# A transformer layer with folded butterflies on one core: where the down side's fold ends, and which engine writes the up side's diagonal matrices

## The chip, the core and the metric

The kernel runs on one core of a Trainium2 chip. The time is device microseconds (us) for one launch. PE is TensorE (matmuls), DVE is VectorE, ACT is ScalarE, POOL is GpSimd, and SP issues most DMAs. Each engine takes its instructions in the order of the program.

## What is computed

A batch of 16 sequences (512 tokens, width 256) goes through causal attention with 16 heads (rotary positions, low-rank additions to wq and wv), a layer norm, a feed-forward block with butterflies, and a second layer norm:

```python
h = einsum('bsd,dh->bsh', x, W_exp) + b_exp          # 256 -> 1024
h = butterfly(h, up_weights, 1024)                   # 10 stages
h = gelu(h + up_bias)
h = butterfly(h, down_weights, 1024)                 # 10 stages
y = einsum('bsh,hd->bsd', h, W_con) + b_con          # 1024 -> 256
```

A butterfly is linear, so the kernel multiplies each of the two into its neighbouring weight matrix once, while the first sequences run: `W_exp` with the up butterfly, `W_con` with the down butterfly. This is the **fold**. After it the feed-forward block is two plain products with the folded weights `wup` and `wdn`.

## The kernel before, in words

The main loop walks through slots `s` from -2 on. Every sequence has 20 slots, in four groups of five (`u` = 0 to 4). From slot 15 on, a slot does two things: the score products of the current sequence's `weights` (line 479, into the PSUM tile `pb`, then exp on ACT at line 493 and a mask on POOL at line 497), and the score products of `largest`, 15 slots ahead (line 421, into `pa`, then row maxima on DVE at line 430). `pb` and `pa` exist once each. So the next slot's `pb` products wait for this slot's exp, and the next `pa` products for this slot's maxima. Behind these come what `others[s]` and `holes` hold for the slot: products with the probabilities (`po`, line 521), projections of later sequences (`pqk`, `pvv`), normalizing (lines 553 and 554), the output projection (`pwo`), and the feed-forward block. Sequence 0 has its first expansion products (`hidden`, line 633, `ph`) in slots 46 to 49, two per slot, its gelus in slot 50, and its first contraction (`contract`, line 660, reads `wdn`) in slot 51.

The fold's tasks are run last in each slot, by a list with a number of tasks due per slot. A task has a `begin`, run up to two tasks ahead, and a second half. The kinds, by side (0 is up, on `ya`; 1 is down, on `wdn`):

- `all_within`: six `multiply_paths` on DVE (line 215) build a matrix of 128x128 per chunk from the factors of seven stages; then eight `within_chunk`, each a matmul (line 219) and an ACT copy (line 222).
- `all_across` by `across_by_products` (up side, stages 7 and 8): per pair of chunks, `begin` writes four diagonal matrices `d` by scaling `ident` (line 255); the second half is four matmuls (line 267) and two ACT copies (line 272).
- `all_across` by `across_chunks` (up side stage 9, down side stages 9, 8, 7): `begin` is two ACT scalings (line 232, tiles `x`, four buffers); the second half is two DVE operations (line 239) on two tensors of SBUF each.
- `up_done` (lines 294 and 295): transposes the folded up side into `wup`.

The up side's `within` runs in slots 2 to 14. Slots 15 to 44 spread the other 44 tasks evenly: 12 across pairs and all 14 `within` tasks of the down side, mixed with 12 across pairs and two small sums of the up side, and four `up_done` at the end. `wup` shares its memory (`yb`) with the down side's factors `factors[1]`, so the down side's `within` has to be over before `up_done` writes.

PSUM for all other products is a ring of three banks (`ps_w`), and `fold`, `pd`, `ptw`, `pt1`, `ph`, `pwo` take turns in it.

Of the kernel before, what the change touches and what calls it, by code (L numbers as in the profile page):

```python
# [11 lines left out]
F32 = mybir.dt.float32  # L12
BF16 = mybir.dt.bfloat16
AF = mybir.ActivationFunctionType
ALU = mybir.AluOpType
PSUM = bass.MemoryType.PSUM

P = 128
# [5 lines left out]
NSP = 7  # L24
# [9 lines left out]
def decoder_layer(  # L34
# [18 lines left out]
    nc = tc.nc  # L53
    B, T, D = x.shape
# [3 lines left out]
    NHC = DHID // P  # L58
    DA = D + 1
    NQ = NC * 2  # L60

    const = ctx.enter_context(tc.tile_pool(name="const", bufs=1))
# [11 lines left out]
    def bank(name, shape):  # L74
        return ps_w.tile(shape, F32, tag="w", name=name)
# [25 lines left out]
    ya = early[:, 0 : NHC * DA].rearrange("p (c d) -> p c d", d=DA)  # L101
    nfac = NHC * (2 * P - 2)
    factors = [early[:, NHC * DA : NHC * DA + nfac], None]
# [4 lines left out]
    coefs = const.tile([P, 2, NS - NSP, NHC, 2], F32, name="coefs")  # L108
    ubias = const.tile([P, NHC], F32, name="ubias")
    wdn = const.tile([P, NHC, D], F32, name="wdn")  # L110
    bias2 = const.tile([P, 2, D], F32, name="bias2")

    yb = const.tile([P, NHC * DA], F32, name="yb")
    wup = yb[:, 0 : NC * DHID].rearrange("p (c e) -> p c e", c=NC)
    factors[1] = yb[:, 0:nfac]


    def load_more(n):
# [86 lines left out]
    def multiply_paths(side, r):  # L205
        m = 1 << r
        if side == 0:
            cur = block(side, r).rearrange("p (c two m) -> p c two m", c=NHC, two=2)
            prev = block(side, r - 1).rearrange("p (c o m) -> p c o m", c=NHC, o=1)
            prev = prev.to_broadcast([P, NHC, 2, m])  # L210
        else:
            cur = block(side, r).rearrange("p (c m two) -> p c m two", c=NHC, two=2)
            prev = block(side, r - 1).rearrange("p (c m o) -> p c m o", c=NHC, o=1)
            prev = prev.to_broadcast([P, NHC, m, 2])
        nc.vector.tensor_tensor(cur, cur, prev, ALU.mult)

    def within_chunk(side, c, y, cols):
        pb = bank(f"fold_{side}_{c}", [P, cols])
        nc.tensor.matmul(
            pb, block(side, NSP - 1)[:, c * P : (c + 1) * P], y[:, c, :], start=True, stop=True  # L220
        )
        nc.scalar.copy(y[:, c, :], pb)
# [23 lines left out]
    def across_by_products(side, s, c, y, cols):  # L246

        pair = (c, c ^ (1 << (s - NSP)))
        parts = {}

        def begin():
            for one in pair:
                d = small.tile([P, 2, P], F32, tag="diag", name=f"d_{side}_{s}_{one}", bufs=4)
                for i in range(2):
                    nc.scalar.activation(
                        d[:, i, :],
                        ident,
                        AF.Identity,
                        scale=coefs[:, side, s - NSP, one, i : i + 1],
                    )  # L260
                parts[one] = d

        def rest():
            for one, other in (pair, pair[::-1]):
                ps = bank(f"pd_{side}_{s}_{one}", [P, cols])
                for i, chunk in enumerate((one, other)):
                    nc.tensor.matmul(
                        ps, parts[one][:, i, :], y[:, chunk, :], start=(i == 0), stop=(i == 1)
                    )
                parts["ps", one] = ps  # L270
            for one in pair:
                nc.scalar.copy(y[:, one, :], parts["ps", one])

        return begin, rest

    def all_across(side, y, cols):

        stages = range(NSP, NS) if side == 0 else range(NS - 1, NSP - 1, -1)
        for s in stages:
            for c in range(NHC):  # L280
                if not c & (1 << (s - NSP)):
                    by = across_by_products if side == 0 and s < NS - 1 else across_chunks
                    yield by(side, s, c, y, cols)

    def mixed(one, two):

        one, two = list(one), list(two)
        keyed = [((i + 0.5) / len(q), n, t) for n, q in enumerate((one, two)) for i, t in enumerate(q)]
        return [t for _, _, t in sorted(keyed, key=lambda k: k[:2])]

    def up_done(d, half):
        pt = bank(f"ptw_{d}_{half}", [P, 4, P])
        for n in range(4):
            nc.tensor.transpose(pt[:, n, :], ya[:, 4 * half + n, d * P : (d + 1) * P], ident)
        nc.vector.tensor_copy(
            wup[:, d, half * 4 * P : (half + 1) * 4 * P],
            pt.rearrange("p n q -> p (n q)"),
        )
# [4 lines left out]
    def all_within(side, y, cols):  # L303
        for r in range(1, NSP):
            yield idle, lambda r=r: multiply_paths(side, r)
        for c in range(NHC):
            yield idle, lambda c=c: within_chunk(side, c, y, cols)

    def fold_tasks():
        def up():  # L310
            yield from all_across(0, ya, DA)
            yield idle, lambda: nc.vector.tensor_add(
                hbias, ya[:, :, D : D + 1].rearrange("p c o -> p (c o)"), ubias
            )
            yield idle, lambda: nc.vector.tensor_add(
                bias2[:, 0, :], bias2[:, 0, :], bias2[:, 1, :]
            )

        def down():
            yield from all_across(1, wdn, D)  # L320
            yield from all_within(1, wdn, D)


        last = [
            (idle, lambda d=d, half=half: up_done(d, half))
            for d in range(NC)
            for half in range(2)
        ]
        return list(all_within(0, ya, DA)), mixed(down(), up()) + last


    def project(b, side, c):
# [352 lines left out]
    per = PER_QUAD * NQ  # L685
    behind = PER_QUAD * BEHIND
    end = B * per + behind
    last = end + 8
# [23 lines left out]
    for b in range(B):  # L712
        s = b * per
# [33 lines left out]
        if b + 2 < B:  # L747

            late = 2 * (b + 3 == B)
# [54 lines left out]
        add(end + 7, finish_tile, z, t)  # L804


    first, second = fold_tasks()
    fold = first + second
    tasks_at = dict(zip(range(2, behind), (0, 1, 2, 3, 4, 4, 5, 5, 5, 6, 9, 11, 14)))
    for s in range(behind, 2 * per + 5):  # L810
        tasks_at[s] = len(first) + -(-len(second) * (s - behind + 1) // (2 * per + 5 - behind))
    ahead = 0
    given = 0
    due = deque()
# [173 lines left out]
```

## Time and profile before

| what | value |
|---|---|
| median of 3 runs | 1359.33 us (1358.64 to 1360.84) |
| profiled execution, its time / its span | 1357.15 us / 1355.4 us |
| PE, DVE, ACT, POOL busy over the span | 1320.3, 925.8, 707.3, 510.9 us |
| first 40:60, 60:80, 100:120 us, PE busy of 20 | 17.85, 16.57, 17.39 us |
| 180:200 us and 220:240 us, PE busy of 20 | 20.00, 19.97 us |
| line 255 (`d`), line 239 (two-tensor operations of the across tasks) | 32 and 32 instructions, all between 56 and 136 us |

PE is busy 97% of the span, and almost all of its idle time lies in the first 170 us, where the fold runs. To read the slots in time: slot 15 begins at 55.4 us (its first `pb` product), slot 26 at 93.4, slot 34 at 122.0, slot 45 at 166.2, slot 50 at 189.8. In the profile, PE's matmuls in fp32 appear as two records each.

### The profile page before, as it was taken

To read this page: it belongs to the slowest core of one execution; us is meant where nothing else is said; L and a number is where in the kernel's file an instruction comes from. 1 tells how busy PE (TensorE), PEld (TensorE's weight loads), DVE (VectorE), ACT (ScalarE), POOL (GpSimd) and SP (SyncE) were. 2 spreads that over 40 slices of the span, in tenths; PEclk is the share of its full clock that TensorE was granted. 3 is DMA by queue.
4 is the path that set the end of the run, shared out by engine and by line. 5 is a ranking of instruction groups with operands and counts; after the bars stand their busy time and mean duration, and the time that the engine had idled before them with its cause. 6 is when DMAs were issued, how large, how long until landed. Compare 5 with 4: busy or idle time off the path is not lost.

```text
span 1355.4 us, 23859 instructions
## 1 busy us (share of the span) xinstructions
PE 1320.3 (97%) x8728; PEld 702.5 (52%) x8728; DVE 925.8 (68%) x2949; ACT 707.3 (52%) x1079; POOL 510.9 (38%) x777
## 2 busy tenths in 40 slices
PE   8898999999999999999999999999999999998998
PEld 4453545455454545555454554545555454554555
DVE  4788757667685766758577685857768685776632
ACT  2575454454646445464645545464554546445643
POOL 3534215344251533425153352515335252531311
PEclk9998999999999999999999999999999999999999
DMA  5311010110102011010110101010110101000000
GB/s 172 120 45 45 22 59 30 40 45 30 68 30 74 30 41 45 30 67 30 67 35 31 57 30 68 30 60 30 40 60 30 68 30 55 30 27 32 30 12 31
DMA packets 45685, 63.49 MB, mean 47 GB/s; under 512 B 5752, under 2 KB 26232, under 8 KB 45568
## 3 DMA queue, kind: packets, MB, share of 16 engines
q1 hardware_dynamic: 41680, 56.42, 11.8%
q10 hardware_dynamic: 3888, 5.55, 1.3%
q8 instruction: 69, 1.13, 0.3%
q14 instruction: 48, 0.39, 0.1%
HBM read 23.40 MB, written 8.91 MB: 24 GB/s over the span
## 4 chain that ended last, share of the span: by engine, by line
PE 84%; DVE 11%; ACT 3%; issue 2%; DMA 0%; POOLq 0%; POOL 0%; DVEq 0%; SPq 0%; ACTq 0%
PE pb L479 19%; PE ph L633 17%; PE py L660 16%; PE po L521 10%; PE pqk L337 8%; DVE junk L430 5%; PE pvv L383 4%; PE pwo L559 3%; PE pa L421 3%; DVE bn L577 1%; PE pb L421 1%; PE pt L616 1%; ACT pT L493 1%; PE pa L479 1%; DVE z L567 1%
## 5 line engine op out<-in xcount | busy, mean ns | idle before, releaser
L430 DVE CUSTOM_DVE_ANT_0 junk<-pa,causal 128x384 bf16<-128x384 f32 (+2 forms) x878 | 438.3, 499 | 235.0 <-PE pa L421 176.1
L493 ACT ACTIVATE pT<-pb 128x1024 f32<-128x1024 f32 (+1 forms) x314 | 293.8, 936 | 377.3 <-PE pa L421 227.6
L497 POOL TENSOR_SCALAR_AFFINE_SELECT pT<-pT 128x256 f32<-128x256 f32 x512 | 202.5, 407 | 733.3 <-ACT pT L493 731.6
L479 PE MATMUL pb<-qz,kz 17*128 17x512 f32 (+2 forms) x1756 | 328.8, 473 | 16.1 <-ACT pT L493 12.1
L421 PE MATMUL pa<-kz,qz 32*128 32x384 f32 (+3 forms) x1756 | 329.2, 474 | 4.2 <-DVE mx L430 4.2
L660 PE MATMUL py<-wdn,h 128*128 128x256 f32 x1024 | 252.1, 391 | 0.0
L479 PEld LDWEIGHTS pb<-qz,kz 17*128 17x128 f32 (+1 forms) x1756 | 142.9, 183 | 179.5 <-issue 82.2
L633 PE MATMUL ph<-x1T,yb 128*128 128x512 f32 x512 | 235.8, 604 | 0.0
L660 PEld LDWEIGHTS py<-wdn,h 128*128 128x128 f32 x1024 | 185.1, 189 | 72.2 <-issue 36.2
L521 PE MATMUL po<-pT,vaug 128*32 128x512 f32 (+3 forms) x2048 | 179.5, 446 | 0.0
L633 PEld LDWEIGHTS ph<-x1T,yb 128*128 128x128 f32 x512 | 92.4, 189 | 122.3 <-issue 97.6
L421 PEld LDWEIGHTS pa<-kz,qz 32*128 32x128 f32 (+1 forms) x1756 | 143.7, 184 | 13.6 <-DVE mx L430 11.2
L553 DVE RECIPROCAL sums<-sums 128x128 f32<-128x128 f32 x128 | 121.1, 946 | 0.0
L337 PE MATMUL pqk<-xT,wqk 128*128 128x512 f32 x256 | 118.5, 613 | 0.0
L646 ACT COPY h<-ph 128x512 f32<-128x512 f32 x84 | 49.2, 585 | 123.2 <-PE ph L633 123.2
L521 PEld LDWEIGHTS po<-pT,vaug 128*32 128x32 f32 x2048 | 47.1, 109 | 102.3 <-issue 78.2
L430 DVE DVE_READ_ACCUMULATOR2_ANT mx<- 128x1 f32 x1024 | 84.5, 82 | 0.0
L337 PEld LDWEIGHTS pqk<-xT,wqk 128*128 128x128 f32 x256 | 48.0, 194 | 61.9 <-issue 57.4
L365 POOL TENSOR_TENSOR swap<-swap,rope_sb 128x512 f32<-128x512 f32 x62 | 79.6, 1283 | 0.0
L602 ACT ACTIVATE z<-z,norm 128x256 f32<-128x256 f32 x128 | 66.7, 589 | 24.6 <-DVE norm L595 24.5
L668 DVE TENSOR_TENSOR z<-py,z 128x256 f32<-128x256 f32 x64 | 27.1, 423 | 74.1 <-PE py L660 73.9
L430 DVE CUSTOM_DVE_ANT_0 junk<-pb,causal 128x256 bf16<-128x256 f32 (+3 forms) x146 | 63.6, 436 | 17.3 <-PE pa L421 4.0
(91 smaller groups left out, 1334.2 us busy)
## 6 DMA issues: line engine op xcount, KB each, us to landing
xT<-in_xT SPq DMA_DIRECT2D x16, 512.0 KB
swap<-qz SPq DMA_DIRECT2D x64, 128.0 KB
swap<-kz SPq DMA_DIRECT2D x64, 128.0 KB
z<-in_x SPq DMA_DIRECT2D x16, 512.0 KB
sums<-x SPq DMA_DIRECT2D x64, 128.0 KB
out_y<-z SPq DMA_DIRECT2D x15, 512.0 KB
x<-x SPq DMA_DIRECT2D x32, 128.0 KB
early<-in_wexpT ACTq DMA_DIRECT2D x1, 1028.0 KB
```

Source lines behind the costliest of these rows:

```text
L337: nc.tensor.matmul(pq, wqk[:, d, e : e + P], xTs[b][:, d, :], start=(d == 0), stop=(d == NC - 1))
L365: engine.tensor_tensor(swap, swap, rope_sb[:, 1, :], ALU.mult)
L421: lambda i=i, rows=rows, at=at, n=n, t=t, ps=ps: nc.tensor.matmul(ps[:, i, at : at + n], q[rows, par, t * P : n], k_[rows, par, 0:n], star ...
L430: lambda i=i, at=at, n=n, t=t, g=g, ps=ps: nc.vector.tensor_tensor_reduce(out=junk[:, 0:n], in0=ps[:, i, at : at + n], in1=causal[:, T - n ...
L479: lambda i=i, rows=rows, at=at, n=n, k=block, ps=ps: nc.tensor.matmul(ps[:, i, at : at + n], kt[rows, par, k * P : (k + 1) * P], qt[rows, ...
L493: nc.scalar.activation(pT[:, heads, 0:n], ps[:, :, at : at + n], AF.Exp)
L497: nc.gpsimd.affine_select(out=diag, in_=diag, pattern=[[0, 2], [1, P]], compare_op=ALU.is_ge, fill=0.0, base=0, channel_multiplier=-1,)
L521: nc.tensor.matmul(po[HG * g : HG * (g + 1), k * P : T], vaugs[b % 2][:, k, NG * c + g, first : first + HG], pT[:, g, at : at + n], start= ...
L553: nc.vector.reciprocal(sums[:, ts], sums[:, ts])
L602: nc.scalar.activation(zs[b][:, t, :], zs[b][:, t, :], AF.Identity, bias=norm[:, 2, t : t + 1], scale=norm[:, 1, t : t + 1],)
L633: nc.tensor.matmul(ph, wup[:, c, hc * P : (hc + 1) * P], state["x1T", b][:, c, :], start=(c == 0), stop=(c == NC - 1),)
L660: nc.tensor.matmul(py, state["h", b][:, hc, t * P : (t + 1) * P], wdn[:, hc, :], start=(hc == 0), stop=(hc == NHC - 1),)
```

## The change

Three things are changed.

1. The down side's list is cut after its eighth task. Stages 9 and 8 stay mixed with the up side in slots 15 to 44. The four pairs of stage 7, the six `multiply_paths` and the eight `within_chunk` (18 tasks) become a third list, run in slots 45 to 49, after the slot's `hidden` products.
2. `factors[1]` gets its own memory, since it now lives while `wup` is written and read.
3. The diagonal matrices `d` are written by POOL instead of ACT.

```diff
-    factors[1] = yb[:, 0:nfac]
+    factors[1] = const.tile([P, nfac], F32, name="factors1")
...
-                    nc.scalar.activation(
+                    nc.gpsimd.tensor_scalar(
                         d[:, i, :],
                         ident,
-                        AF.Identity,
-                        scale=coefs[:, side, s - NSP, one, i : i + 1],
+                        coefs[:, side, s - NSP, one, i : i + 1],
+                        None,
+                        ALU.mult,
                     )
...
-        def down():
-            yield from all_across(1, wdn, D)
-            yield from all_within(1, wdn, D)
-
-
-        last = [
+        down = list(all_across(1, wdn, D))
+        late = down[2 * NHC // 2 :] + list(all_within(1, wdn, D))
+        up_last = [
             (idle, lambda d=d, half=half: up_done(d, half))
             for d in range(NC)
             for half in range(2)
         ]
-        return list(all_within(0, ya, DA)), mixed(down(), up()) + last
+        return list(all_within(0, ya, DA)), mixed(down[: 2 * NHC // 2], up()) + up_last, late
...
-    first, second = fold_tasks()
-    fold = first + second
+    first, second, third = fold_tasks()
+    fold = first + second + third
     tasks_at = dict(zip(range(2, behind), (0, 1, 2, 3, 4, 4, 5, 5, 5, 6, 9, 11, 14)))
-    for s in range(behind, 2 * per + 5):
-        tasks_at[s] = len(first) + -(-len(second) * (s - behind + 1) // (2 * per + 5 - behind))
+    needed = 2 * per + 5
+    for s in range(behind, needed):
+        tasks_at[s] = len(first) + -(-len(second) * (s - behind + 1) // (needed - behind))
+    for s in range(needed, needed + 5):
+        tasks_at[s] = len(first + second) + -(-len(third) * (s - needed + 1) // 5)
```

So slots 15 to 44 now hold 26 tasks instead of 44. The four pairs of stage 7 fall into slot 45, four `multiply_paths` into slot 46, the last two and one `within_chunk` into slot 47, four `within_chunk` into slot 48 and three into slot 49. The instructions of an engine that come after slot 50 stand in the same order as before.

## Prediction

> **What bounds the kernel now.** I read the engines' busy time in 40 slices first: PE is at 9 tenths everywhere but in the first five slices. The change touches only slots 14 to 50, so I cut their time into four stages at slot starts and read the busy time of each engine per stage (columns: stretch, its length, then PE, weight loads, DVE, ACT, POOL, granted PE clock, DMA).
>
> ```profile
> 55.40:93.40 38.00, 32.40 (x256) 17.86 (x255) 27.79 (x90) 32.49 (x77) 9.67 (x19) 1.00 0.08 27
> 93.40:122.00 28.60, 24.71 (x180) 11.71 (x179) 26.97 (x76) 15.88 (x31) 14.98 (x22) 0.99 0.18 63
> 122.00:166.20 44.20, 41.19 (x281) 22.10 (x281) 31.92 (x105) 21.50 (x38) 11.24 (x22) 0.85 0.07 23
> 166.20:189.80 23.60, 23.60 (x141) 10.24 (x140) 14.72 (x43) 8.70 (x12) 5.47 (x9) 1.00 0.10 34
> ```
>
> Then the chain of waits of the first and the last stage, as shares by line:
>
> ```profile
> by line: PE pd L267 19.9%; PE pb L479 13.7%; ACT pT L493 13.2%; ACT d L255 11.6%; ACT x L232 9.0%; PE po L521 6.8%; PE pqk L337 5.0%; PE pa L421 4.6%; DVE junk L430 4.5%; issue 4.1%; ACT early L272 4.1%; ACT early L222 1.4%; ACT x L540 1.3%
> ...
> by line: PE ph L633 61.5%; PE pb L479 20.0%; PE po L521 10.9%; PE pt L616 4.3%; PE pb L421 1.7%; PE pa L421 1.2%; PE ptw L294 0.6%; PE pa L479 0.1%
> ```
>
> Four stages, four limits. A (slots 15 to 25) swings between ACT and PE. B (26 to 33) is DVE's: 26.97 of 28.60 us. C (34 to 44) is PE's at a clock of 0.85. D (45 to 49), where 18 tasks go, is PE alone, without any idle time. The change takes work from three stages with holes and puts it into the one without.
>
> **The change, stage by stage.**
>
> A. ACT loses most of the 32 diagonal writes: four take 1.17 us in the chain, so 0.3 each, and they hold 11.6% of 38.0, 4.4 us of the chain. It also loses the scalings of the down pairs, now spread thinner (9.0%, 3.4 us). Together 7.8 us, but PE has the same work as before here (six product pairs, 1.93 us each), is busy 32.40, and can lose 5.6 us of idle at most. Of that, slots with little PE work keep some: the loop from `pb` product over exp to the next `pb` product takes 2.3 us (slot 18, 65.6 to 67.8), and slots 16, 21, 22 and 25 hold 1.1 to 2.2 us of PE work, so some 3 us stay. Gain 2 of the 2.6 left; bounds 0 and 3.5. POOL's write is not in the trace. Nearest rows: a mask of 256 elements at 0.407 us, a two-tensor operation of 512 at 1.27. I take 0.3 (bounds 0.2 and 0.6); 32 are 10 us on a POOL with 28 us free in A. Each matrix is begun one slot or more before its product, so it costs nothing; if POOL were late, a product pair would wait up to 4 x 0.6. The masks queue behind these writes, but their `po` comes a slot later.
>
> B. DVE loses the six path products (0.18 + 0.33 + 1.70 + about 2.0, 4.2 us) and a stage 7 pair (1.53), and gains two stage 8 pairs and one up pair (3 x 0.95): net 2.9 less. Against it: two product pairs come a slot or two earlier, into slots 26 and 27, beside `pqk` (1.92) and `po`, where PE is then the limit (1.2 + 1.9 + 1.9 = 5.1 us instead of 3.0 in slot 26; 27 stays at 4.0). Before, the pair in slot 29 hid under DVE's normalizing; that wait stays. So about +2 in slots 26 to 29 and -1 in 30 to 33, where exp and the maxima set the pace as soon as the path products are gone: **+1**, bounds -2.9 and +2.
>
> C. Eight `within` products leave. They hold 3.6 us of the chain here, two slots of them at half clock. The up pairs done earlier give some 0.6. Gain 4.2. The clock is the open part: it was at half rate for 13.7 us (121.7 to 128.5, 135.4 to 138.8, 162.7 to 166.1). Half rate can cost at most half of that, 6.8, and half of it again where PE is not the limit: without it the gain would be 4.2 + 3.3 = 7.5. If one more window of 3.4 us fell to half rate, as products with 128 rows leave slots 34 to 41, it would be 4.2 - 1.7 = 2.5.
>
> D. PE is full, so eight `within` products add 8 x 0.45 (two records at the full-clock row's 0.44 per product): **+3.6**, with nothing to hide them. Then two waits that the trace does not show yet. Here is slot 45 to 46 (start, length, engine, line):
>
> ```profile
> 168.18 0.69 DVE L430 CUSTOM_DVE_ANT_0 junk<-pa,causal 128x512 bf16<-128x512 f32 x1
> ...
> 168.79 1.28 DVE L617 COPY x1T<-pt 128x512 f32<-128x512 f32 x2
> ...
> 169.03 2.36 POOL L621 TENSOR_TENSOR z<-z,bias 128x1024 f32<-128x1024 f32 x1
> ...
> 170.11 0.69 DVE L430 CUSTOM_DVE_ANT_0 junk<-pa,causal 128x512 bf16<-128x512 f32 x1
> ...
> 173.62 0.59 PE L479 MATMUL pb<-qz,kz 17*128 17x384 f32 x2
> ```
>
> The first wait: the eight operations of stage 7 come on DVE between the copy to `x1T` and the maxima of slot 46, so the maxima start not at 170.1 but after the eight, and slot 47's `pa` products wait for them. How long do eight take beside POOL's L621?
>
> ```profile
> L239 DVE SCALAR_TENSOR_TENSOR wdn<-wdn,coefs,x x24: 472/478/1492, 58.0 to 98.1; 128x256 f32<-128x256 f32 x24
> ```
>
> The row gives 478 ns, but a maximum of 1492. Those slow ones lie beside POOL's rotary products: the pair from 97.09 took 1.53 us while POOL's L367 ran to 97.94. The Trainium skill's page "SBUF — State Buffer", section "SBUF: two separate sides", has the rule: a VectorE operation with two SBUF inputs and a GpSimd operation that reads SBUF exclude each other for a whole instruction. By the row's median alone the eight end at 170.1 + 3.8 = 173.9, and the maxima at 175.4; by the rule the first waits for L621 at 171.4, the eight end at 175.2, the maxima at 176.7. PE is ready at 173.6: 1.8 us or **3.1** lost. I take the rule, since the slow rows agree with it. ACT's last two pairs of scalings wait for DVE to free their `x` buffers, and slot 46's exp stands behind them; it ends near 174.9, so DVE is later. The same rule argues against the writes on POOL in A, where DVE has 10 us idle to absorb it.
>
> The second: after those maxima DVE has the copy of `ph` (0.69), four path products (1.2), slot 47's maxima (2.1), normalizing (1.24) and the last two path products (2.0): from 176.7 to 184.0. PE, restarted at 176.7, does 1.1 + 1.0 + 3.6 and stands at the first `within` at 182.5: **1.5** lost. The other seven have their copies (0.37) on an ACT that is free two thirds of this stage. Bounds of both waits: 0 and 6.
>
> A stall can also halve the clock:
>
> ```profile
> 60.30:63.70 3.40, 2.15 (x25) 0.95 (x25) 2.51 (x9) 3.32 (x9) 0.67 (x1) 1.00 0.02 5
> 118.30:121.70 3.40, 1.84 (x16) 0.99 (x16) 3.26 (x9) 1.02 (x1) 1.36 (x4) 1.00 0.06 22
> 121.70:125.10 3.40, 3.12 (x20) 1.61 (x24) 2.25 (x8) 0.66 (x2) 0.97 (x2) 0.50 0.00 0
> ```
>
> After a window with 1.84 us of PE work the clock fell to 0.50, after one with 2.15 it did not. The skill ("TensorE: Matmul & The Clock Gate", "Part 1: The HAM clock gate") says that an idle window of about 3.4 us is needed. By that rule a 3.1 us stall costs nothing more; by the row, one half-rate window, up to 1.7. I take 0 and keep 1.7 for the range.
>
> Sum: -2.0 + 1.0 - 4.2 + 3.6 + 3.1 + 1.5 = **+3.0 us**. On the profiled execution, 1357.15 us, that is 1360.1; its time lies 2.2 under the median of the runs, so 1359.33 + 3.0 = **1362.3** for the median.
>
> **The rivals.** (1) *The holes close and the waits of D don't come*: the clock stays up in C (-7.5), DVE's relief counts in B (-2.9), and D costs the products and half of the waits (+5.9). -2.0 - 2.9 - 7.5 + 5.9 = -6.5: 1352.8; with only half of the clock's part, 1355. For it: 13.7 us at half rate follow DVE's stretch in B. Against: C loses products with 128 rows. The sign turns once the waits of D are under 1.6 us with the rest as summed. (2) *DVE's backlog in D is the bound*: waits of 6 us and a half-rate window (1.7), C gains 2.5 only: -2 + 1 - 2.5 + 3.6 + 6 + 1.7 = +7.8: 1367.1. For it: DVE gets 8 us in five slots with 14.72 of 23.6 busy. (3) *Nothing nets out*: the products cost in D what they cost in C, and the waits equal what A gains: 1359 to 1360.
>
> **How the numbers follow.** Forecast and its surroundings (1360 to 1365) 0.48, rival 1 0.22, rival 2 0.15, rival 3 0.15. The range is 1354.5 to 1368. About 0.2%, 2.7 us, is what can be told from no change. Rival 1 gives most of the chance of faster, 0.20; rival 3 and the lower part of the forecast give 0.28 for the same; the rest and rival 2 give 0.52 for slower.
>
> **What would show it.** Slot 26 begins near 91.4 and slot 34 near 121; slot 45 at 161, not 166. Then slot 47's `pa` waits for line 430 some 3 us, PE's first `fold` of the down side waits for line 215, and slot 50 begins near 193, some 32 us after slot 45 where 23.6 were enough. No wait of a `pd` product for POOL. The forecast is wrong if slot 47 starts on time, if the clock reads 1.00 through C, or if anything after slot 50 differs.

## The result and the profile after

The changed kernel takes 1372.95 us (median of 6 runs, 1369.48 to 1377.58). The kernel before took 1358.99 beside it (6 runs, 1355.32 to 1361.32). The ratio is 1.0107, with a 95% interval of 1.0082 to 1.0132. The forecast was 1362.3, at most 1368: slower was right, the size was not. The profiled execution of the changed kernel took 1373.98 us with a span of 1372.2.

The page shows in 40 slices where the difference lies. Each digit is a share in tenths; the second row is the clock granted to PE.

```profile
PE   8998999999999999999999999999999999998998
...
PEclk8997799999999999999999999999999999999999
```

Slices 4 and 5 (103 to 172 us) have 7 tenths of the clock. PE's busy row shows nothing of it, since a matmul at half rate counts as busy for longer (eight `po` products below: 1.94 us instead of 1.07). The same four stages as before, cut at the changed kernel's slot starts, which are the first `pb` products (columns: stretch, length, then PE, weight loads, DVE, ACT, POOL busy with the number of instructions, granted PE clock, DMA share, GB/s):

```profile
56.30:94.50 38.20, 34.47 (x254) 18.85 (x255) 20.32 (x74) 20.26 (x38) 23.75 (x45) 0.96 0.08 26
94.50:127.00 32.50, 27.52 (x173) 12.96 (x173) 25.66 (x72) 16.87 (x30) 18.04 (x25) 0.84 0.16 55
127.00:172.40 45.40, 41.29 (x269) 20.36 (x269) 35.61 (x112) 18.84 (x31) 13.09 (x24) 0.74 0.06 22
172.40:205.40 33.00, 31.48 (x153) 14.51 (x152) 21.36 (x56) 14.74 (x29) 5.50 (x10) 0.90 0.07 25
```

One boundary of the kernel before has to be set right. Its slot 34 begins at 120.39 us by its first `pb` product; 122.0 is the first `pa` product of that slot. Cut at the same event as above, its stages B and C are:

```profile
93.40:120.40 27.00, 24.00 (x176) 11.40 (x175) 25.47 (x68) 15.88 (x31) 13.39 (x19) 1.00 0.19 66
120.40:166.20 45.80, 41.90 (x285) 22.40 (x285) 33.42 (x113) 21.50 (x38) 12.84 (x24) 0.85 0.06 22
```

Stage B has nearly as many PE instructions as before (173 against 176) and takes 5.5 us longer, at a clock of 0.84 instead of 1.00. Stage C has fewer of them (269 against 285), but at 0.74 instead of 0.85 it is only 0.4 us shorter. In stage D, where the work went, the clock was 1.00 and is now 0.90.

By stage, in us; "at half rate" is the time in which the clock record of the profile shows 0.5:

| stage | predicted | after - before | half rate, before | half rate, after |
|---|---|---|---|---|
| up to slot 15 | 0 | +0.8 | 3.4 | 10.2 |
| A, slots 15 to 25 | -2.0 | +0.3 | 0 | 3.4 |
| B, 26 to 33 | +1.0 | +5.5 | 0 | 10.2 |
| C, 34 to 44 | -4.2 | -0.4 | 13.7 | 23.9 |
| D, 45 to 49 | +8.2 | +9.4 | 0 | 6.8 |
| from slot 50 on | 0 | +1.1 | 1.5 | 5.0 |
| sum | +3.0 | +16.8 | 18.6 | 59.5 |

The half-rate windows lie on a grid of 3.4 us. This is how one long stretch of them looks in the changed kernel, window by window (columns as above):

```profile
124.80:128.20 3.40, 1.95 (x28) 1.47 (x24) 3.13 (x12) 2.02 (x4) 2.94 (x5) 1.00 0.12 43
128.20:131.60 3.40, 2.55 (x23) 0.65 (x19) 3.02 (x10) 2.45 (x5) 1.89 (x4) 0.50 0.01 2
131.60:135.00 3.40, 3.40 (x18) 1.05 (x20) 2.82 (x5) 1.20 (x3) 1.61 (x2) 0.50 0.00 0
135.00:138.50 3.50, 2.92 (x10) 1.29 (x12) 3.14 (x7) 2.30 (x4) 1.86 (x3) 0.50 0.20 75
138.50:141.90 3.40, 3.40 (x24) 1.68 (x20) 2.42 (x8) 1.02 (x1) 0.05 (x1) 0.50 0.00 0
141.90:145.30 3.40, 3.40 (x16) 1.65 (x12) 2.09 (x8) 0.37 (x1) 0.72 (x2) 0.50 0.00 0
145.30:148.70 3.40, 2.11 (x28) 1.24 (x26) 2.31 (x10) 1.05 (x2) 0.77 (x2) 1.00 0.00 0
```

The first row lies in slots 33 and 34 and leaves PE 1.95 us of work in 3.40, all of it in products with 16 or 32 rows; the next row is at 0.50. Before, half rate set in at the same place too, but for two windows (121.7 to 128.5); now it is five, in the slots from 34 on that lost the `within` products. The clock comes back only after a window in which PE was busy throughout (3.40 of 3.40), and not after each such window. The last row, 2.11 us of work, starts the next stretch at 148.7. The stretch in B is new: slot 29 holds 2.27 us of PE work here and 4.51 before, because the list, with 26 instead of 44 tasks for the same slots, has no product due there.

In D the wait that was foreseen for slot 47 is there. Here is the timeline of slots 46 to 48 (start, length, engine, line, operation, and in brackets the idle time before it and what ended it):

```profile
175.60 2.35 POOL L621 TENSOR_TENSOR z<-z,bias 128x1024 f32<-128x1024 f32 x1
...
176.29 4.71 DVE L239 SCALAR_TENSOR_TENSOR wdn<-wdn,coefs,x 128x256 f32<-128x256 f32 x8
...
178.33 1.71 ACT L232 ACTIVATE x<-wdn,coefs 128x256 f32<-128x256 f32 x4 [2.76 <-DVE wdn L239]
...
179.94 1.00 ACT L493 ACTIVATE pT<-pb 128x1024 f32<-128x1024 f32 x1
...
180.99 0.92 PE L479 MATMUL pb<-qz,kz 17*128 17x384 f32 x4 [1.00 <-ACT pT L493]
...
182.40 0.61 PE L421 MATMUL pa<-kz,qz 32*128 32x384 f32 x2 [0.49 <-DVE mx L430]
...
184.01 1.94 PE L521 MATMUL po<-pT,vaug 128*32 128x512 f32 x8
...
185.88 5.57 PE L633 MATMUL ph<-x1T,yb 128*128 128x512 f32 x8
...
191.28 0.59 PE L219 MATMUL fold<-wdn,factors 128*128 128x256 f32 x2
```

The eight DVE operations take 4.71 us beside POOL's L621; ACT's next scalings wait 2.76 us for them, exp comes behind these, and PE waits 1.00 for exp and 0.49 for the maxima. After that pause the clock is halved from 182.8 to 189.7: the next `po` takes 1.94 us and the next eight `ph` products 5.57, where slot 47 of the kernel before had 1.07 and 3.70.

### The profile page after: what moved, and what is told of

Its sections match the earlier page's. It is cut to its first block, busy times and chain, and to the rows that moved or that the text cites. A ratio compares the mean times of both kernels' runs of the same rounds, so it can differ in the third digit from the quotient of the medians.

```text
span 1372.2 us, 23873 instructions
## 1 busy us (share of the span) xinstructions
PE 1336.2 (97%) x8728; PEld 709.5 (52%) x8728; DVE 927.9 (68%) x2949; ACT 699.4 (51%) x1047; POOL 530.4 (39%) x809
## 4 chain that ended last, share of the span: by engine, by line
PE 86%; DVE 10%; ACT 2%; issue 2%; DMA 0%; POOLq 0%; POOL 0%; DVEq 0%; ACTq 0%
PE pb L479 19%; PE ph L633 17%; PE py L660 16%; PE po L521 10%; PE pqk L337 8%; DVE junk L430 5%; PE pvv L383 4%; PE pwo L559 3%; PE pa L421 3%; DVE bn L577 1%; PE pb L421 1%; PE pd L268 1%; PE pt L616 1%; ACT pT L493 1%; DVE z L567 1%
## 5 line engine op out<-in xcount | busy, mean ns | idle before, releaser
L479 PE MATMUL pb<-qz,kz 17*128 17x512 f32 (+2 forms) x1756 | 334.5, 479 | 20.0 <-ACT pT L493 16.4
L421 PE MATMUL pa<-kz,qz 32*128 32x384 f32 (+3 forms) x1756 | 335.7, 482 | 1.6 <-DVE mx L430 1.6
L521 PE MATMUL po<-pT,vaug 128*32 128x512 f32 (+3 forms) x2048 | 182.6, 452 | 0.0
L337 PE MATMUL pqk<-xT,wqk 128*128 128x512 f32 x256 | 121.9, 627 | 0.0
L668 DVE TENSOR_TENSOR z<-py,z 128x256 f32<-128x256 f32 x64 | 27.1, 423 | 74.1 <-PE py L660 73.9
```

Of the source, the lines that this page charges most:

```text
L337: nc.tensor.matmul(pq, wqk[:, d, e : e + P], xTs[b][:, d, :], start=(d == 0), stop=(d == NC - 1))
L421: lambda i=i, rows=rows, at=at, n=n, t=t, ps=ps: nc.tensor.matmul(ps[:, i, at : at + n], q[rows, par, t * P : n], k_[rows, par, 0:n], star ...
L479: lambda i=i, rows=rows, at=at, n=n, k=block, ps=ps: nc.tensor.matmul(ps[:, i, at : at + n], kt[rows, par, k * P : (k + 1) * P], qt[rows, ...
L521: nc.tensor.matmul(po[HG * g : HG * (g + 1), k * P : T], vaugs[b % 2][:, k, NG * c + g, first : first + HG], pT[:, g, at : at + n], start= ...
```

## The experiments

Two theories stood after the result. **H**: the products with 128 rows that left slots of stages B and C kept the clock up; without them it falls, so putting any such products back makes the kernel faster. **R**: ACT's scalings wait for their `x` buffers, since the down side's across tasks now follow each other closely; the waits hold up exp, and with it PE. For R spoke a view of the changed kernel, the waits of line 232 (us, times):

```profile
  DVE early L239: 6.3, 4
  DVE wdn L239: 6.3, 3
```

### Which part of the change: e1_pool_only and e2_move_only

The first is the kernel before with line 255 on POOL, the second the changed kernel with line 255 back on ACT:

```diff
-                    nc.scalar.activation(d[:, i, :], ident, AF.Identity, scale=coefs[...])
+                    nc.gpsimd.tensor_scalar(d[:, i, :], ident, coefs[...], None, ALU.mult)
```

> The kernel before, with only the diagonal matrices written by GpSimd. Theory R (the slowdown comes from the moved list: across tasks now stand next to each other, so the third pair's ACT scalings wait for a buffer of the ring of four x tiles until VectorE has done the first pair, exp stands behind them, PE idles, and the PE clock halves): here the list is as before, so no such wait; ACT loses 9.4 us of work in slots 15 to 29, 1355 to 1360 us, ratio 0.997 to 1.001. Rival T (the writes on GpSimd, 0.605 us each instead of 0.3, hold up the masks and the products): 1363 us or more, with pd products or po products waiting for GpSimd for several us.

> The changed kernel, with the diagonal matrices written by ACT again; the list is moved. Theory R: nearly the whole slowdown stays, 1369 to 1376 us, ACT's scalings wait for VectorE some 12 us in all, and the granted clock is at half rate for 30 us or more of the first 210. Rival T: most of it goes, 1362 us or less.

POOL's writes alone: 1360.43 us, ratio 0.9992 (0.9974 to 1.0009). The moved list alone: 1370.89 us, 1.0087 (1.0059 to 1.0116), with B and C at the same lengths (32.50, 45.30) and the same half-rate time (10.2, 23.9) as in the changed kernel. So the move is the cause, and POOL's writes change nothing that can be measured. They are twice as long as assumed, and a product hardly ever waits for them (the changed kernel; ns are min/median/max, waits are us, times):

```profile
L255 POOL TENSOR_SCALAR d<-ident,coefs x32: 601/605/876, 56.2 to 98.6; 128x128 f32<-128x128 f32 x32
...
who waited for it (us, times):
  PEld pd L268: 0.8, 1
```

### The ring of x buffers: e3_after_ring6 and e4_before_ring6

Six `x` buffers instead of four (and one `mT` buffer instead of two, for the space), in the changed kernel and, as a control, in the kernel before:

```diff
-tag="cross", name=f"x_{side}_{s}_{one}", bufs=4
+tag="cross", name=f"x_{side}_{s}_{one}", bufs=6
...
-tag="mT", name=f"mT_{b}_{c}")
+tag="mT", name=f"mT_{b}_{c}", bufs=1)
```

> The changed kernel with six x buffers instead of four (and one mT buffer instead of two, to make room). Theory R: the waits of ACT's scalings for VectorE fall from 12.6 us to under 4, exp is on time, stages B and C (slots 26 to 44) lose 5 us or more and half-rate time falls from 44 us to 25 or less: 1363 to 1367 us, what is left being the slots 45 to 49. Rival H (the clock halves because the products with 128 rows left slots 34 to 41, whatever ACT waits for): half-rate time stays at 35 us or more in slots 26 to 49 and the time at 1369 us or more.

> The kernel before with six x buffers and one mT buffer. Control: in the kernel before ACT's scalings waited for VectorE 0.5 us in all, so both theories expect no change, within 2 us of 1359.

The waits of line 232 fell from 12.6 us to this, in the view of e3_after_ring6:

```profile
  DVE wdn L239: 1.9, 1
```

But the time stayed: 1373.66 us, 1.0101 (1.0075 to 1.0127), with 27.3 us at half rate in C. The control took 1360.75, 0.9998. So R does not explain the time of the changed kernel. It is not gone for good: one such wait of 1.6 us shows once the clock is held (slot 32 of e11_after_wide, below), and no run has both six buffers and a held clock.

### Products put back: e5_dummies_back and e6_dummies_dense

The changed kernel with added products of 128 rows and 256 columns, whose result nobody reads, at the ends of some slots: eight where the moved `within` products had been (e5), or twenty where stages B and C have holes (e6).

```diff
+WARM = {34: 2, 36: 1, 37: 1, 38: 1, 39: 1, 40: 1, 41: 1}
...
+    def keep_warm(s):
+        for n in range(WARM.get(s, 0)):
+            pd = bank(f"warm_{s}_{n}", [P, D])
+            nc.tensor.matmul(pd, ident, wqk[:, 0, 0:D], start=True, stop=True)
...
+        keep_warm(s)
```

In e6 `WARM` has two each for slots 29, 30, 32 to 36, 38, 40 and 43.

> The changed kernel plus eight dummy products of 128x256 with 128 rows, nobody reads them, in slots 34 (two) and 36 to 41 (one each), where the kernel before had its within products. It adds work and removes none. Theory H (the PE clock halves in stretches of low PE work, as full-row products left slots 30 to 41): half-rate time in slots 34 to 44 falls from 24 us to about 15, and that stage is no longer than 45.5 us though 3.5 us of PE work came in; in all 1368 to 1373 us. Rival W (the clock follows from PE waiting for late VectorE and ACT work, and dummies add their time): half-rate time stays at 20 us or more there, the stage takes 48 us or more, 1375 us or more in all.

> The changed kernel plus two such dummy products in each of slots 29, 30, 32 to 36, 38, 40 and 43, where PE has little to do (9 us of added PE work). Theory H: half-rate time in slots 26 to 44 falls from 34 us to 10 or less, stages B and C together from 78 us to 72 or less, 1364 to 1368 us in all. Rival W: half-rate time there stays at 25 us or more and the time rises to 1376 us or more.

Stage C of e5_dummies_back, then stages B, C and D of e6_dummies_dense:

```profile
132.20:176.10 43.90, 40.80 (x289) 21.29 (x289) 35.67 (x112) 20.06 (x33) 13.34 (x24) 0.86 0.07 23
```

```profile
96.30:127.00 30.70, 26.96 (x189) 14.10 (x189) 25.85 (x72) 16.77 (x30) 18.02 (x25) 1.00 0.17 58
127.00:165.10 38.10, 36.64 (x293) 20.64 (x293) 35.03 (x112) 18.65 (x31) 13.07 (x24) 1.00 0.08 26
165.10:195.90 30.80, 28.41 (x152) 13.34 (x152) 21.25 (x56) 14.81 (x29) 5.48 (x9) 1.00 0.08 27
```

With eight products more, C is 1.5 us shorter than in the changed kernel, and its half-rate time falls from 23.9 to 12.3 us. The total does not show it (1371.18, 1.0085, with an interval of 1.0052 to 1.0117; the profiled run had more half rate before slot 26). With twenty, no window of B, C or D is at half rate: B and C together take 68.8 us instead of 77.9, and the kernel takes 1364.93, 1.0047 (1.0032 to 1.0062). More work, less time: H holds. What no run separates is the rows from the PE time, since every added product has 128 rows; the windows of the traces, in the last section, speak for the rows.

### Only the within products late: e7_within_late and e10_within_late_dense

The four pairs of stage 7 and all six path products go back into the mix (the expectation of e10 counts one of these as late; the edit leaves none); e10 adds two products each in slots 29, 30, 32, 33, 35, 36, 38, 40 and 43.

```diff
-        late = down[2 * NHC // 2 :] + list(all_within(1, wdn, D))
+        within = list(all_within(1, wdn, D))
+        down, late = down + within[: NSP - 1], within[NSP - 1 :]
...
-mixed(down[: 2 * NHC // 2], up())
+mixed(down, up())
```

> The changed kernel with only the eight within products late (slots 45 to 49); the four pairs of stage 7 and the six path products are back in the mix of slots 15 to 44. What the summed waits of slots 45 to 49 say: no wait of slot 47's pa products for VectorE and none of the first within product for the path products, so slots 45 to 49 take 23.6 + 3.6 = 27 to 28 us instead of 33.0, without half-rate time. Stage B is near the 28.6 us of the kernel before, as the list is long again. 1361 to 1365 us. Rival P (the products themselves and their banks make slots 45 to 49 slow): 31 us or more there.

> Only the eight within products (and one path product) of the down side late, d on POOL, and 18 added 128-row products in slots 29 to 43. Clock theory: no window at half rate in slots 26 to 44, slots 34 to 44 in 38 to 39 us, slots 45 to 49 in 27 to 28, total within 0.5% of the kernel before, 1356 to 1360. Rival (moving the within products costs C something besides the clock): slots 34 to 44 over 42 us without half rate, total over 1364.

Stages B, C and D of e7_within_late, then C of e10_within_late_dense:

```profile
96.70:128.90 32.20, 26.03 (x176) 12.23 (x175) 27.23 (x72) 16.88 (x32) 18.61 (x28) 0.94 0.17 56
128.90:177.00 48.10, 43.06 (x273) 21.83 (x273) 35.19 (x115) 19.05 (x30) 13.51 (x24) 0.72 0.06 21
177.00:204.30 27.30, 27.14 (x153) 12.93 (x152) 14.74 (x43) 11.34 (x21) 5.51 (x9) 1.00 0.09 30
```

```profile
133.50:175.60 42.10, 39.90 (x294) 22.17 (x293) 34.52 (x113) 17.06 (x26) 12.97 (x23) 0.89 0.07 24
```

D came as expected: 27.36 us, so eight `within` products cost 3.8 there (predicted 3.6), with no wait. The rest was a miss. Without fillers (the added products) B took 32.1 us, where the kernel before takes 27.0, C 48.1 with 27.1 at half rate, and the kernel 1373.52 (1.0097, 1.0072 to 1.0122): as long as the changed kernel, though D lost 5.6 us. So the clock is lost without the other ten tasks leaving too. That the eight products alone do it is not shown, since the shorter list also spreads its other tasks over other slots. The fillers of e10 did not hold the clock either: 9.3 us at half rate are left in C, after a window (129.2 to 132.6) with 2.16 us of PE work. That the tasks lie in other slots than in the kernels for which the fillers were chosen is the likely reason, and was not tested. e10 took 1367.78 (1.0059). Stage B was 5 us longer than in the kernel before with the same fillers, almost without half rate; why was not followed up.

### The wait in D: e9_late_bias

e6_dummies_dense with POOL's bias addition (line 621) for sequence 0 behind slot 48 instead of beside the eight DVE operations:

```diff
         if c == NC - 1:
-            nc.gpsimd.tensor_tensor(zs[b], zs[b], bias2[...], ALU.add)
+            if b > 0:
+                lift(b)
...
         keep_warm(s)
+        if s == 48:
+            lift(0)
```

Here `lift` is that addition.

> The run with 20 added products on the changed kernel (1364.93 us, slots 45 to 49 in 30.78 us, no half rate there), with POOL's bias addition to sequence 0's z (line 621) put behind slot 48 instead of beside stage 7's eight DVE operations. Prediction's theory (the shared port holds the first of the eight until POOL is done): the eight take 3.8 us instead of 4.70, none of them over 0.6 us, and slots 45 to 49 take 29.9 or a little less; total 1364. Rival (the eight are slow for another reason, or slot 47 waits for exp on ACT alone): the eight still have one of 1.4 us or more, or slots 45 to 49 stay at 30.8.

The `wdn` operations of line 239 (here L240), first in stage D of e6_dummies_dense, then in the same stage of e9_late_bias (min/median/max in ns):

```profile
L240 DVE SCALAR_TENSOR_TENSOR wdn<-wdn,coefs,x x8: 471/472/1931, 169.0 to 173.2; 128x256 f32<-128x256 f32 x8
```

```profile
L240 DVE SCALAR_TENSOR_TENSOR wdn<-wdn,coefs,x x8: 475/476/477, 170.1 to 172.9; 128x256 f32<-128x256 f32 x8
```

The one of 1931 ns is gone, and D takes 29.32 us instead of 30.78. The prediction's port rule (the Trainium skill's page "SBUF — State Buffer", "SBUF: two separate sides") holds: 1931 ns beside POOL, 477 at most without it, and 1.5 us of the stage (1.3 was the difference between rule and row in the prediction). The kernel took 1361.88 (1.002, 1.0007 to 1.0032).

### The kernel before with products added, and the change at a held clock: e8, e11, e12

e8_before_dummies is the kernel before with e10's fillers; e12_before_wide adds one product each in slots 0 to 13, 16, 18 and 20 to 22; e11_after_wide is the changed kernel with the fillers of e12 and two more in slot 34 and one each in 46 and 47.

> The kernel before plus two dummy products in each of slots 29, 30, 32, 33, 35, 36, 38, 40 and 43. Theory H: its 13.4 us of half-rate time in slots 34 to 44 fall to 5 or less and the time falls by 2 to 5 us, to 1355 to 1358. Rival W: the dummies add up to 8 us, 1362 us or more.

> The changed kernel with added 128-row products in nearly every slot that has a hole (0 to 13, 16, 18, 20 to 22, 29, 30, 32 to 36, 38, 40, 43, 46, 47). Clock theory: at most one window of 3.4 us at half rate in the first 210 us; against the before kernel with the same products, it is longer by the cost of slots 45 to 49 alone, 7 to 9 us, total 1358 to 1364. Rival: over 10 us longer, so something besides the clock is lost before slot 45.

> The kernel before with added 128-row products also in slots 0 to 13, 16, 18 and 20 to 22. Clock theory: the 13.7 and 3.4 us at half rate that were left before slot 26 go, 19 products of 0.44 us are mostly hidden: 1350 to 1354, faster than with the products in slots 29 to 43 alone (1355.39). Rival (early slots are full, so added products only cost): 1357 to 1364.

e8 took 1355.39 us, 0.9968 (0.9953 to 0.9982), and e12 1354.22, 0.9963 (0.9947 to 0.998): both faster than either kernel of this case. e12 came out 0.2 us above what was expected, and is not to be told apart from e8. e11 took 1363.21, 1.0026 (1.0016 to 1.0037). In the profiled runs of e11 and e12 no window before slot 50 is at half rate. Their stages A to D, e11_after_wide and then e12_before_wide:

```profile
54.50:91.90 37.40, 34.77 (x266) 19.67 (x265) 20.33 (x74) 20.40 (x39) 22.01 (x42) 1.00 0.08 27
91.90:122.60 30.70, 26.94 (x189) 14.07 (x189) 25.84 (x72) 16.74 (x30) 17.99 (x25) 1.00 0.17 58
122.60:160.70 38.10, 36.65 (x295) 20.71 (x295) 34.99 (x112) 18.68 (x31) 13.07 (x24) 1.00 0.08 26
160.70:191.90 31.20, 29.28 (x157) 14.06 (x158) 21.24 (x56) 14.77 (x28) 5.47 (x9) 1.00 0.08 26
```

```profile
56.20:94.60 38.40, 35.17 (x268) 19.40 (x267) 27.56 (x90) 32.53 (x77) 9.67 (x19) 1.00 0.08 26
94.60:122.00 27.40, 27.12 (x191) 13.53 (x190) 25.43 (x68) 15.94 (x31) 13.36 (x20) 1.00 0.19 65
122.00:161.90 39.90, 38.62 (x306) 22.95 (x305) 33.45 (x113) 19.70 (x35) 12.77 (x24) 1.00 0.07 25
161.90:185.50 23.60, 23.60 (x141) 10.20 (x140) 14.73 (x43) 10.01 (x16) 5.46 (x9) 1.00 0.11 35
```

At a held clock the change costs -1.0 in A, +3.3 in B, -1.9 in C and +7.7 in D (by the slot starts), 8.1 us in the four; without fillers it was 14.8. So 6.7 us of these stages' loss come back with the clock. In the ratios the loss is 1.07% without fillers and 1.0026 - 0.9963 = 0.63% with them, that is 14.5 and 8.6 us of 1359, and 6 for the clock, by the intervals some 2 to 10. So somewhat under half of the loss is the clock, with a wide margin. e11 has four more fillers than e12 (up to 4 x 0.44 = 1.8 us of PE), which belong to the 8.1 and not to the change.

Of the 3.3 us in B, 2.1 are slot 26, whose PE work rises from 2.98 to 5.12 us with the pair that comes into it. Another 1.6 are slot 32 (4.78 us instead of 3.14). There ACT's scaling waits for DVE, exp stands behind it, and PE waits for exp, as R had it (e11_after_wide):

```profile
117.36 0.87 DVE L240 SCALAR_TENSOR_TENSOR early<-early,coefs,x 128x257 f32<-128x257 f32 x2
...
117.92 0.91 ACT L233 ACTIVATE x<-early,coefs 128x257 f32<-128x257 f32 x2 [2.11 <-DVE early L240]
...
118.74 1.00 ACT L494 ACTIVATE pT<-pb 128x1024 f32<-128x1024 f32 x1
...
119.80 0.59 PE L480 MATMUL pb<-qz,kz 32*128 32x384 f32 x2 [1.57 <-ACT pT L494]
```

## Why the prediction was wrong

**The step that failed is the clock's**, and with it C's gain of 4.2. The sum takes the granted clock of the kernel before as given. It has nothing for the clock in A and B and takes 0 in D, and for C one more window at half rate "as products with 128 rows leave slots 34 to 41" was the bad end. The mechanism was named for C, and its size missed by far: not one window more but three in C (23.9 against 13.7 us), three in B, two in D and one in A. For B and C together the prediction had -3.2; measured are +5.1, and +1.5 at a held clock. The working priced the products that leave by their own duration; what they did for the clock of the products around them was left at one window. e5 shows it: eight such products back in C take away 11.6 us of half rate. e7 fits, with 30.7 us at half rate in B and C against 13.7 before.

The clock is not the whole miss: at a held clock the change still costs 8 (up to 1.8 of it by e11's four more fillers), not 3. **C** then gains 1.9, or 2.7 if the two more fillers of slot 34 are counted at their full 0.44 each. Whether the bare stage would gain 4.2 at full clock stays open, since without fillers no version kept it.

**B**, +1.0: it was +5.5, and +3.3 at a held clock, above the upper bound of +2. The +2 of slots 26 to 29 was right (slot 26 as worked out: 5.12 us instead of 2.98). The -1 of slots 30 to 33 was not: at a held clock they take 13.7 us instead of 12.1, and slot 32 alone is 1.6 longer, by the wait for `x` that the working put at nothing. The other 2.2 are the clock. The working looked at pairs that come into slots 26 and 27; it did not look at the slots that they left. Slot 29, which has 2.27 us of PE work in 4.95, was in the new order of the list to be seen. The stages of the prediction were cut at 122.0 instead of 120.39, too; that moves 1.6 us between B and C and nothing in their sum.

**A**, -2.0: at a held clock -1.0, with `d` on ACT (e2) -1.4, in the changed kernel +0.3 with one window at half rate. POOL's write is 0.605 us, not 0.3: the upper bound was right. That it costs nothing was right (e1, 0.9992), with 0.8 us of waiting in all; but ACT's relief brought nothing that can be measured either.

**D**, +8.2: the mechanism and nearly the size were right. At full clock (e6) it is 30.78 - 23.54 = +7.2: 3.8 for the products (by e7; predicted 3.6) and 3.4 for the waits (predicted 3.1 + 1.5). The second wait came there too, 0.88 us of the first `within` product for the path products; in the changed kernel, where half rate slowed PE, it did not. Slot 47 waited for exp first and for the maxima second; the prediction had put exp 1.3 us late as well, and called DVE the later one. The port rule was right and is worth 1.5 us (e9). The question that was decided wrongly is whether the stall halves the clock. The Trainium skill's rule (page "TensorE: Matmul & The Clock Gate", "Part 1: The HAM clock gate"), which asks for an idle window, gave 0, and the row of this kernel's own trace gave up to 1.7; measured are two windows and 32.96 - 30.78 = 2.2 us. The measurement decides for the row: PE was idle for 1.00 us in one piece there, with 1.9 us of work in the window from 179.4. But the row was read by PE time alone: the window with 1.84 us that lost the clock had no product with 128 rows, the one with 2.15 that kept it had 0.98 us of them.

**Outside the stages**: +0.8 before slot 15 and +1.1 after slot 50, where nothing was to differ. (Of PE's 35.1 us without work in the kernel before, 20.3 lie in the first 170 us and 14.9 behind them, so the later part is not free of idle time either.) The order of the engines' work after slot 50 is the same, but one window near 1330 fell to half rate; the same happens near the end in e8 and e11 and not in e12. The half-rate time before slot 15 is between 0 and 13.7 us in the profiled runs of this study, on nearly the same code. Such windows may explain the spread of the runs; that is argued, not shown.

Of the rivals, the second had the nearest total (1367.1), but by waits of 6 us in D that did not come. The first, the clock kept up in C, is what the fillers made by force.

## What to carry to other kernels

Before a product is taken out of a stage with holes, ask what it does for the clock of that stage: read the granted clock of each window of 3.4 us beside its PE time, that of products with 128 rows above all, and add up the same PE time for the slots of the order planned. A tile of work moved from under-filled slots to a full stretch costs its whole duration there, and can cost as much again where it was (e7: 3.8 us in D, 7.4 in B and C). Where a stage loses its clock to holes, products that compute nothing can be worth their time: 18 of them made the kernel before 0.3% faster.

## What the runs showed of the hardware

- The clock went to half rate after grid windows of 3.4 us with 1.1 to 2.4 us of PE work, and twice after one of 2.9 (all ten times that it fell between 15 and 215 us in the two kernels). Windows of 2.1 in the kernel before, and of 1.93 in e6, kept full rate. So PE time alone does not decide it.
- The rows of the products count. Between 15 and 1340 us of all fourteen profiled runs, no window with more than 1.6 us of PE work in products of 128 rows lost the clock. Of the windows with almost nothing else in them, it fell after all ten with 1.33 to 1.59 us (1.59 in e3) and after none with 1.71 (e12) or more. The two windows of 2.9 us that lost it had only 0.80 and 0.99 us of such products, the rest with 16 to 32 rows. What these thinner products add is open: a window with 0.57 us of 128 rows and 2.23 of them (128.5 in the kernel before) kept full rate.
- In all ten half-rate stretches of the first point the last window at half rate was one in which PE was busy throughout. Where the slots have holes even at half rate, a stretch goes on: 17.1 us here, 23.9 in e7.
- POOL's scaling of a 128x128 tile by a column took 605 ns in the median of 32; ACT's records of the same work have 395 ns.
